# Unread matrix products issued on TensorE in the planned gaps of the first stage of a one-core layer kernel

## The chip, the core and the metric

The kernel runs on one core of one Trainium2 chip. The metric is the device time of one execution in microseconds (us), median of several runs. Every time below comes from the runs or from one profiled execution of the kernel before the change.

## What is computed

Sixteen sequences of 256 tokens with 128 features pass through four residual layers, each on a layer-normed input:

```
x = x + attn_a(layernorm(x))      # einsum('blmh,blhd->blhd'): the softmax row sums to 1, so it is
                                  # (x @ w_v.T + b_v) @ w_out.T + b_out
x = x + ffn(layernorm(x))         # 8 experts, top 2 of x @ gate_w, softmax over the two logits
x = x + ssm(layernorm(x))         # selective scan: 16 states, softplus delta, cumulative decays
x = x + ffn(layernorm(x))         # the same experts and gate again
```

The expert layer is, for each token, the sum over its two experts of the weight times `relu(x @ w1[e]) @ w2[e]`, with `w1[e]` 128x512 and `w2[e]` 512x128, all in float32.

## The kernel before

**Blocks and sets.** The 4096 tokens are 8 blocks of 512. `FIRST` groups them into sets for the first expert layer, ([0], [1], [2,3], [4,5], [6,7]), and `SECOND` into sets for the second. A set is routed as a whole: every token's row, scaled by its gate weight, is scattered by indirect DMA (`scatter`, POOL, line 807) to a slot of its expert in a DRAM buffer `slots`; the experts then read dense tiles from there, and `gather` (line 821) brings the results back by the same indices.

**What one block goes through before its first scan.** `attention`: TensorE (PE) transposes the loaded `xT` into token rows (`ps_b<-ident,xT`), ACT or DVE copies them to `x`, DVE takes the layer-norm statistics, POOL raises to the power -1/2 (`rstd`) and adds the bias (`x<-x,batt`), PE multiplies `xT` by the folded attention matrix (`ps_b<-wat,xT`), DVE adds the product to `x`. `gate`: statistics again, `xn`, PE transposes (`ps_b<-ident,xn`), copy to `xnT`, PE makes 8 gate logits per token (`ps_b<-gw_s,xnT`, 8 columns wide), copied to `lg`. `choose` and `route`: a row of small DVE operations finds the two experts (`oh`, `both`); PE counts the tokens ahead of each one (`ps_b<-both,before` and `ps_b<-both,onesb`, bf16); DVE makes the slot numbers (`rank`, `m`, `sf`, `to`), and POOL scatters. `experts`: a tile `xs` is fetched by SP, transposed on PE, copied to `xsT`; four up products `ps_b<-xsT,w_s` (192 columns in the first set) go through a ReLU on ACT or DVE to `h`; four down products accumulate in the one bank `ps_y<-h,w_s`; then copies, transposes and the write to `ys`. `mixer` holds the selective scan.

**Order.** No scheduler decides at run time. Every operation is recorded as a `Job` with a cost per engine; `Plan.forward` lists them on a model clock by ranks kept in `ORDER`, which gives each job an engine, a start and a buffer; `Plan.order` returns the jobs sorted by that start, and the loop at the end of `tile_layers` emits them. Each engine then works through its own list strictly in that order, waiting on semaphores where a value is not ready. In this plan's model a transposition takes PE 0.12 us and a float32 product of 128 columns 0.42 us.

**PSUM.** There are two banks of kind `b` of 512 columns, shared by nearly all short PE results, so a PE instruction often waits for the copy that empties its bank; one bank `y`, of which the experts use at most the first `NMAX` = 384 columns; and the banks `s`, `B`, `C` of the scan.

**Names the change touches.** `Plan.order` (the list it returns), the loop at line 1441 on, the bank `kinds["y"][0]`, and the constants `ones_d` (128x128, 1/128 everywhere) and `blank` (128x128, zero). Both constants are made by POOL at the start; no engine but PE gets another instruction or another order.

Of the kernel before, what the change touches and what calls it, by code (L numbers as in the profile page):

```python
# [21 lines left out]
TB = 512  # L22
# [12 lines left out]
JOIN = 2  # L35
ACC = 0
POOLED = (3,)
SUMS = 0
DENSE = ([], [])

# [144 lines left out]
class Plan:  # L185
# [160 lines left out]
    def order(self):  # L346

        self.prepare()
        d = zlib.decompress(base64.b85decode(ORDER))
        n = len(d) // 2  # L350
        assert n == len(self.jobs)
        at, rank = 0, []
        for lo, hi in zip(d[:n], d[n:]):
            at += int.from_bytes((lo, hi), "little", signed=True)
            rank.append(-at)
        end, start, way, buffer = self.made = self.forward(rank)
        for h, b in zip(self.homes, buffer):
            if b is not None:
                h.buffer = b
        order = sorted(range(n), key=lambda i: (start[i], i))  # L360
        return [(self.jobs[i], next(w for w in self.jobs[i].ways if w[0] == way[i])) for i in order]


@with_exitstack
# [229 lines left out]
def tile_layers(  # L594
# [33 lines left out]
    nc = tc.nc  # L628
    NTOK = xT.shape[1]
    NB = NTOK // TB  # L630
    NE, _, FF = w1.shape
    NFC = FF // P
# [15 lines left out]
    NMAX = max(c * n for _, c, n in every)  # L648
    MOST = -(-max(t * c * n for t, c, n in every) // P) * P

    plan = Plan()
# [6 lines left out]
    kinds = {}  # L658
# [78 lines left out]
    def either(*ways, extra=0.0, **order):  # L737

        made = []
        for e, name, a, k in ways:  # L740
            views = [x for x in (*a, *k.values()) if isinstance(x, View)]
            took = cost(e, name, views) + extra
            out = k["out"] if "out" in k else a[0]
            held = locking(e, name, out, [x for x in views if x is not out] + (
                [out] if sum(x is out for x in views) > 1 else []
            ))
            made.append((e, took, call(getattr(engines[e], name), a, k), held))
        _, _, a, k = ways[0]
        out = k["out"] if "out" in k else a[0]
        ins = [x for x in (*a, *k.values()) if isinstance(x, View) and x is not out]  # L750
        return plan.job(made, [out], ins, **order)
# [10 lines left out]
    def copy(out, in_, pool=False, **order):  # L762
        ways = [("ACT", "copy", (out, in_), {}), ("DVE", "tensor_copy", (out, in_), {})]
        if pool:
            ways.append(("POOL", "tensor_copy", (out, in_), {}))
        return either(*ways, **order)
# [61 lines left out]
    def filled(name, shape, value, dtype=F32):  # L828
        t = new(name, shape, dtype)
        G.memset(t, value)  # L830
        return t
# [18 lines left out]
    def load_experts():  # L850
# [21 lines left out]
        out=ident, in_=ident, pattern=[[-1, P]], compare_op=ALU.not_equal, fill=1.0, base=0,  # L872
        channel_multiplier=1,
    )
    ones_d = filled("ones_d", [P, P], 1.0 / P)
# [6 lines left out]
    blank = filled("blank", [P, P], 0.0)  # L882
# [5 lines left out]
    for q in range(3):  # L888
# [5 lines left out]
        out=before, in_=onesb, pattern=[[1, P]], compare_op=ALU.is_gt, fill=0.0, base=0,  # L894
# [5 lines left out]
        out=upto[:, P:L], in_=upto[:, P:L], pattern=[[-1, P]], compare_op=ALU.is_ge, fill=0.0, base=0,  # L900
# [388 lines left out]
    def mixer(b, r, m):  # L1289
# [31 lines left out]
        )  # L1321
        if SUMS:

# [24 lines left out]
        for n in range(0, NS, 2):  # L1348
# [29 lines left out]
            )  # L1378
            if n // 2 in POOLED:
                V.scalar_tensor_tensor(th, th, 1.0, pC, ALU.add, ALU.mult)  # L1380
# [61 lines left out]
    gap = sbuf.tile([1, 1], F32, tag="gap", name="gap")  # L1442
    last = None
    with tc.manual_schedule():
        for job, way in plan.order():
            if way[0] == "POOL":
                if job.key is not None and job.key == last:
                    nc.gpsimd.memset(gap, 0.0)
                last = job.key
            way[2]()  # L1450


    most = kept_s.tile([1, 1], F32, tag="most", name="most")
# [53 lines left out]
```

## Time and profile before

| | us |
|---|---|
| median of 3 runs | 724.63 (724.1 to 726.0) |
| the profiled execution's own time | 724.93 |
| its span, first to last instruction | 723.2 |
| first selective scan starts | 128.7 |
| first expert tile is transposed on PE | 54.64 |

Mean granted TensorE clock: 0.917 of full speed.

| stretch, us | PE busy | DVE busy | ACT busy | POOL busy | granted PE clock |
|---|---|---|---|---|---|
| 0 to 54.6 | 32.36 | 33.88 | 16.37 | 28.68 | 0.69 |
| 54 to 68.2 | 11.07 | 7.13 | 5.93 | 10.42 | 0.64 |
| 130 to 640 (510 us) | 462.36 | 462.57 | 395.51 | 305.04 | 0.94 |

How to read it: busy time is summed per engine; all kernel lines of the planned part show as line 710, the helper through which every recorded operation is called, so the groups are told apart by their tiles. A float32 product is recorded as two matmul records, a transposition as one. The granted clock is 1.00 or 0.50 at any moment; in between are means. From 0 to about 54 us the weights and the first tokens arrive, the first blocks are routed, and no expert runs yet; from 54 to 128 us the first experts run; from then on scans and experts overlap to the end.

### The profile page before, as it was taken

The numbers are of one execution on the slowest core, as the hardware profiler recorded it, in microseconds if no ns is written. First come the engines' busy times: TensorE is split into PE (matmuls) and PEld (weight loads), VectorE is DVE, ScalarE is ACT, GpSimd is POOL, SyncE is SP. The second block draws the span as 40 slices with busy tenths as digits, with TensorE's granted clock in tenths as the row PEclk, the third lists the DMA queues.
The fourth block names the chain that finished last, engine by engine and source line by source line (L and its number), as shares of the span: only waits on it lengthen the run. The fifth ranks groups of instructions, "written<-read, shape, count | busy, mean of one in ns | idle before, by whom it ended". The sixth has DMA issues, their size and how long they took to land. (4 is left out here: it accounts for less than half of the span.)

```text
span 723.2 us, 8786 instructions
## 1 busy us (share of the span) xinstructions
PE 624.5 (86%) x2598; PEld 390.6 (54%) x2598; DVE 554.6 (77%) x1038; ACT 487.7 (67%) x996; POOL 414.5 (57%) x490
## 2 busy tenths in 40 slices
PE   5477999799999769899888889887999999999970
PEld 4366877465645226555344554333555555578860
DVE  4765448999998798899999898998998998740120
ACT  2243538988867797679989668689867775355440
POOL 5367771397075458677953852864037787314743
PEclk9557999999999878799999999889999999999995
DMA  7931331221330001321122101110112512213342
GB/s 228 334 116 52 94 100 42 67 59 47 88 85 20 1 28 48 112 67 33 35 68 79 56 26 30 58 58 23 51 31 80 156 56 70 83 46 103 100 136 76
DMA packets 76373, 55.05 MB, mean 76 GB/s; under 512 B 8064, under 2 KB 69152, under 8 KB 76320
## 3 DMA queue, kind: packets, MB, share of 16 engines
q1 hardware_dynamic: 66464, 37.35, 17.8%
q0 software_dynamic: 8192, 16.79, 7.8%
q8 instruction: 22, 0.36, 0.2%
q10 hardware_dynamic: 1664, 0.29, 0.2%
q14 instruction: 31, 0.25, 0.1%
HBM read 27.09 MB, written 27.32 MB: 75 GB/s over the span
## 5 line engine op out<-in xcount | busy, mean ns | idle before, releaser
L710 PE MATMUL ps_b<-xsT,w_s 128*128 128x330 f32 (+3 forms) x640 | 211.0, 438 | 15.2 <-ACT h L710 6.8
L710 PE MATMUL ps_y<-h,w_s 128*128 128x330 f32 (+3 forms) x640 | 214.1, 425 | 3.4 <-ACT yT L710 2.2
L821 POOL DMA_INDIRECT yy<-ys,of x128 | 124.6, 973 | 100.7 <-DMA ys<-yr 38.5
L807 POOL DMA_INDIRECT slots<-row,to x128 | 126.7, 990 | 79.4 <-issue 22.1
L710 ACT ACTIVATE h<-ps_b 128x384 f32<-128x384 f32 (+2 forms) x234 | 110.2, 475 | 88.7 <-PE ps_b L710 85.4
L710 PEld LDWEIGHTS ps_b<-xsT,w_s 128*128 128x128 f32 x640 | 115.3, 197 | 74.1 <-ACT h L710 24.6
L710 DVE TENSOR_TENSOR_SCAN w<-decay,ps_B 128x1024 f32<-128x1024 f32 x64 | 145.8, 2279 | 0.2
L710 PEld LDWEIGHTS ps_y<-h,w_s 128*128 128x128 f32 x640 | 109.9, 195 | 44.8 <-issue 11.8
L710 ACT ACTIVATE th<-later,lneps,ha_s 128x512 f32<-128x512 f32 x128 | 100.1, 809 | 5.1 <-DVE th L710 2.9
L710 ACT ACTIVATE decay<-delta,nea 128x510 f32<-128x510 f32 x128 | 86.7, 714 | 4.7 <-DVE w L710 3.5
L710 DVE TENSOR_TENSOR ps_B<-du,ps_B 128x1024 f32<-128x1024 f32 x64 | 78.2, 1222 | 13.4 <-PE ps_B L710 13.2
L710 DVE SCALAR_TENSOR_TENSOR ps_C<-th,ps_C 128x1024 f32<-128x1024 f32 x56 | 68.2, 1219 | 6.9 <-PE ps_C L710 6.8
L710 PE MATMUL ps_s<-th,wsh_s 128*128 128x512 f32 x128 | 69.6, 636 | 3.8 <-POOL th L710 3.8
L710 DVE TENSOR_TENSOR th<-ps_C,w 128x1024 f32<-128x1024 f32 x56 | 67.9, 1213 | 0.2
L710 POOL TENSOR_TENSOR th<-th,th 128x1024 f32<-128x1024 f32 x20 | 47.2, 2360 | 29.5 <-DVE th L710 27.2
L710 POOL TENSOR_TENSOR rstd<-var,root 128x8 f32<-128x8 f32 (+1 forms) x20 | 28.2, 1412 | 52.1 <-DVE var L710 49.5
L710 PEld LDWEIGHTS <-sel 96*128 96x128 bf16 x256 | 25.9, 103 | 58.9 <-issue 48.3
L710 PE MATMUL ps_B<-pieces,sel 96*128 96x512 bf16 x128 | 42.0, 401 | 10.4 <-DVE w L710 10.3
L710 PE MATMUL ps_b<-ident,yT 128*110 128x128 f32 (+3 forms) x208 | 43.6, 279 | 2.8 <-ACT h L710 0.8
L710 PE MATMUL ps_b<-ident,xs 110*128 110x110 f32 (+3 forms) x208 | 38.9, 278 | 7.1 <-ACT h L710 3.2
L710 PE MATMUL ps_C<-pieces,sel 96*128 96x512 bf16 x128 | 41.7, 405 | 3.2 <-DVE th L710 3.0
L710 PEld LDWEIGHTS ps_b<-ident,xs 110*128 110x128 f32 (+3 forms) x208 | 26.6, 148 | 25.9 <-ACT h L710 8.5
(161 smaller groups left out, 810.6 us busy)
## 6 DMA issues: line engine op xcount, KB each, us to landing
slots<-blank SPq DMA_DIRECT2D x3, 1536.0 KB
xs<-slots SPq DMA_DIRECT2D x24, 192.0 KB
ys<-yr SPq DMA_DIRECT2D x24, 192.0 KB
w_s<-in_w SPq DMA_DIRECT2D x16, 256.0 KB
xs<-slots SPq DMA_DIRECT2D x24, 165.0 KB
ys<-yr SPq DMA_DIRECT2D x24, 165.0 KB
xT<-in_xT SPq DMA_DIRECT2D x8, 256.0 KB
slots<-row,to POOLq DMA_INDIRECT x128, 2.3
```

Of the source, the lines that this page charges most:

```text
L710: return lambda: f(*[real(x) for x in a], **{n: real(x) for n, x in k.items()})
L807: inst = nc.gpsimd.indirect_dma_start(out=real(out), out_offset=bass.IndirectOffsetOnAxis(ap=real(rows), axis=0), in_=real(in_), in_offset ...
L821: nc.gpsimd.indirect_dma_start(out=real(out), out_offset=None, in_=real(in_), in_offset=bass.IndirectOffsetOnAxis(ap=real(rows), axis=0), ...
```

## The change

`Plan.order` now returns, with each job, the time that PE stands idle just ahead of it on the model clock, for jobs that start before 110 us there. The loop emits, ahead of such a job, one 128x128x128 float32 product for each 0.24 us of that idle time: `ones_d` times `blank`, into the 128 columns of the bank `y` that no expert uses. Nobody reads it. While an expert's sum is open in the bank `y` (`summing`), none is emitted. Everything else keeps its order.

```diff
+WARM = 110.0
@@ Plan.order
         order = sorted(range(n), key=lambda i: (start[i], i))
-        return [(self.jobs[i], next(w for w in self.jobs[i].ways if w[0] == way[i])) for i in order]
+
+        idle, free = {}, 0.0
+        for i in order:
+            if way[i] == "PE":
+                idle[i] = start[i] - free if start[i] < WARM else 0.0
+                free = start[i] + self.jobs[i].took["PE"]
+        return [
+            (self.jobs[i], next(w for w in self.jobs[i].ways if w[0] == way[i]), idle.get(i, 0.0))
+            for i in order
+        ]
@@ tile_layers
     with tc.manual_schedule():
-        for job, way in plan.order():
+        spare, summing = kinds["y"][0][:, NMAX:TB], 0
+        for job, way, idle in plan.order():
+
+            for _ in range(0 if summing else int(idle / 0.24)):
+                nc.tensor.matmul(
+                    out=spare, lhsT=ones_d.real(), rhs=blank.real()[:, 0 : TB - NMAX],
+                    start=True, stop=True,
+                )
             if way[0] == "POOL":
                 if job.key is not None and job.key == last:
                     nc.gpsimd.memset(gap, 0.0)
                 last = job.key
             way[2]()
+            if way[0] == "PE" and any(h.kind == "y" for h in job.homes):
+                summing = (summing + 1) % NFC
```

In the built program this puts 132 products into PE's list, in 26 runs:

| ahead of | products |
|---|---|
| first transposition of the first block | 15 |
| the next transpositions and weight products | 3, 2, 1, 2 |
| `wat` products of the third and the fourth block | 6 and 22 |
| transposition of the first `xn` | 13 |
| its logits, and two weight products | 3, 1, 1 |
| counting products of the first set's route | 22 |
| transposition of the second `xn` | 15 |
| the next `xn` | 3, 1 |
| transposition of the fifth block's `xT` | 7 |
| the rest up to the first expert tile | 1, 3, 1, 1, 3 |
| first up products, first down product | 2, 2 |
| two later places, among the first set's experts | 1, 1 |

The first of them waits for POOL (the two constants). One of the later two carries the wait for ACT that the up product behind it had. DVE, ACT, POOL and SP have the same instructions in the same order as before.

## The prediction

> **What bounds the kernel now.** I read the page's slices first, then the stretches cut at the moments where the granted clock flips, then the order of time of PE alone, then of all engines. From 130 to 640 us DVE and PE are each busy 462 of 510 us and the change puts nothing there, so what counts is how much earlier or later the first expert stage hands over. The slices show where the clock is low:
>
> ```profile
> PE   5477999799999769899888889887999999999970
> PEclk9557999999999878799999999889999999999995
> ```
>
> A slice is 18 us. The third and fourth digits of PEclk cover 36 to 72 us, with PE busy in seven to nine tenths: there the clock may set the pace. Cut at the flips (duration, PE busy with records, then PEld, DVE, ACT, POOL, clock, DMA):
>
> ```profile
> 12.04:15.46 3.42, 2.94 (x13) 2.68 (x13) 2.10 (x10) 1.09 (x4) 3.00 (x4) 1.00 0.97 253
> 15.46:18.87 3.41, 1.41 (x13) 1.22 (x11) 3.33 (x9) 0.00 (x0) 2.44 (x2) 1.00 1.03 317
> ...
> 42.76:46.17 3.41, 3.41 (x18) 3.41 (x17) 1.40 (x11) 0.77 (x2) 2.81 (x5) 0.50 0.18 58
> 46.17:49.59 3.42, 2.70 (x17) 2.09 (x16) 2.46 (x19) 0.98 (x3) 1.29 (x3) 0.50 0.12 38
> 49.59:53.00 3.41, 3.39 (x23) 2.96 (x21) 2.78 (x16) 2.23 (x6) 1.93 (x2) 0.50 0.40 118
> 53.00:56.41 3.41, 1.91 (x10) 1.25 (x10) 3.37 (x15) 1.86 (x5) 1.88 (x3) 1.00 0.01 3
> ...
> 63.24:66.65 3.41, 3.41 (x12) 3.41 (x11) 1.64 (x11) 0.76 (x2) 2.07 (x4) 0.50 0.18 58
> ```
>
> The clock moves in steps of 3.41 us and each step follows the one before. Half turns to full after nearly full PE stretches (49.59, 63.24), full is lost after 1.41 and 1.91 us busy; later 2.04 us (from 128.09) holds it and 1.82 (from 131.51) loses it. The stretch from 42.76 is full of gate products 8 columns wide and does not raise it: narrow products hardly count. Up to 15.46 the view says 1.00, but single transpositions last as long there as at 0.50 later (four in 1.08 us at 4.31, four in 1.09 at 27.60); I take that part as half clock too.
>
> ```profile
> 19.26 2.07 PE L710 MATMUL ps_b<-wat,xT 128*128 128x128 f32 x8 [2.39 <-DVE x L710]
> 24.44 2.08 PE L710 MATMUL ps_b<-wat,xT 128*128 128x128 f32 x8 [3.11 <-DVE x L710]
> 27.60 1.09 PE L710 MATMUL ps_b<-ident,xn 128*128 128x128 f32 x4 [1.08 <-DVE x L710]
> ...
> 34.72 0.19 PE L710 MATMUL ps_b<-both,before 128*128 128x40 bf16 x1 [1.64 <-DVE p L710]
> ...
> 37.91 1.12 PE L710 MATMUL ps_b<-ident,xn 128*128 128x128 f32 x4 [2.92 <-ACT xn L710]
> ...
> 43.41 3.42 PE L710 MATMUL ps_b<-gw_s,xnT 128*128 128x8 f32 x16
> 46.68 1.09 PE L710 MATMUL ps_b<-ident,xT 128*128 128x128 f32 x4
> ...
> 54.64 0.39 PE L710 MATMUL ps_b<-ident,xs 96*128 96x96 f32 x2 [0.68 <-ACT x L710]
> ```
>
> In brackets stands PE's idle time ahead: these are the gaps the new products go into, and they are not the plan's gaps.
>
> **Price of one product.** It is two records. At half clock 16 records take 3.42 us: 0.213 each, 0.43 a product. At full clock the 192-column records of 72 to 78 us come in pairs 0.325 apart, 0.163 each; by columns 128/192 of that is 0.108, and four transpositions of 128 columns in 0.60 us (104.89), the last one 0.27 long, give 0.11. The bounds are 0.11 and 0.163 a record; I take 0.11, the same width: 0.22 a product, 29 us for 132.
>
> **Walk through the front, clock held at full.**
> - 15 ahead of the first block: they start when `blank` is written (2.28 + 0.20) and, at half clock until one 3.41 us step is full, end between 7.2 and 8.9 instead of the 4.31 at which the first block landed. What hides it is ACT, which makes its first copy of a block only at 9.94, behind its table load, and 3.46 us of idle DVE ahead of 10.55: 0 to +0.5. Without that cover it would be +3 to +4.6.
> - 3, 2, 1, 2 and 6: 1.3 us or less each, in gaps of 0.3 to 2.4: nothing.
> - 22 ahead of the fourth block's `wat`: the third block's eight records take 0.9 from 19.26; 20.2 + 4.9 = 25.1 against 24.44, but at full clock these eight end at 26.1 against 26.5. Nothing.
> - 13 ahead of the first `xn`: 26.1 + 2.9 = 29.0 against 27.60. Transpositions 0.6 against 1.09, eight gate records 1.05 against 1.87: logits at 31.2 as before. Even.
> - 22 ahead of the route: from 32.5 to 37.4 in a gap of 1.64, so the count starts 2.7 late. Behind it on DVE stand `rank`, the slot numbers and the next block's `xn`; 0.73 us of DVE idle ahead of `rt` absorbs some, so scatters start 2.0 late (39.6) and, at 1.27 each, end at 49.7 instead of 47.7. SP's fetch, queued behind them, goes from 48.96 to 51. PE asked for that tile at 54.64, so this is hidden; about 2 us of slack are left.
> - 15 and 3 ahead of the next `xn`: 40.9 against 37.91, 3.0 late. From there PE is the pace: 36 records up to 46.83, all at half clock before. At full the 16 gate records take 1.8 instead of 3.42; the last logits come at 46.5 + 0.2 against 46.86. Regained.
> - 7 ahead of the fifth block's `xT` (46.68, no gap before): 1.6 us. The copy that empties its bank, and with it the last product of the second route, comes 0.55 later (DVE `rank` 49.95 against 49.42). Behind that on DVE are statistics, for which POOL waits at 51.07; its three additions stretch DVE, and the first up product (55.54) moves as much. The 3, 1, 1, 3, 2 and 2 after it lie in gaps of 0.3 to 0.7: nothing.
>
> Sum: +0.55, up to +1.0 with the first item.
>
> **What the clock gives in the first experts.** Rows of PE from 57 to 68:
>
> ```profile
> 57.04 1.01 PE L710 MATMUL ps_y<-h,w_s 128*128 128x192 f32 x2 [0.58 <-ACT h L710]
> 60.46 1.65 PE L710 MATMUL ps_b<-xsT,w_s 128*128 128x192 f32 x4 [0.41 <-ACT xsT L710]
> 62.69 1.01 PE L710 MATMUL ps_y<-h,w_s 128*128 128x192 f32 x2 [0.58 <-ACT h L710]
> 64.77 3.57 PE L710 MATMUL ps_b<-xsT,w_s 128*128 128x192 f32 x14
> ```
>
> Between 57.04 and 62.69 the chain is four down records, two transposed tiles, four up records, with an ACT copy after each group; at 0.163 instead of 0.32 a record it is 3.8 instead of 5.65 long. From 62.69 to 68.17 twenty wide records run, bound by PE; at full 3.3 to 3.6 (the ReLUs of 0.49 now pace them) instead of 5.5. Together 3.8. PE is then the pace until 91 and POOL's scatters, closed up from 79.6 to 97, have 4.6 us of waits before 79.6 to give back, so it carries to the first scan. Net with the clock held: 0.55 - 3.8 = -3.2.
>
> **Where the clock is lost again.** A long dip of wide products costs one step at half rate.
> - Dip A: the 6 products end near 16.8 and PE waits until 19.26, 2.4 us. A step that holds most of it has 1.0 to 1.4 us of work, like the one that lost the clock at 18.87. About half of all positions of the step do. Then 3.4 us of the 22 products run at half: +1.7.
> - Dip B: from 42.0 to 46.5 there are some 1.1 us of wide records; the rest are gate products. Steps starting from 41.7 to 44.0 lose it: two in three. Then the 7 products cost up to 3.0 instead of 1.6, transpositions and gate records double: the second route comes 1.6 to 3.3 late instead of 0.55, and the experts may start at half clock, which takes up to a third off the 3.8.
>
> Held -3.2; A alone -1.5; B alone +2.2 - 3.8 x 0.85 = -1.0; both about +0.7, with the late end of B +2.5.
>
> The Trainium skill, page "TensorE: Matmul & The Clock Gate", section "Why this matters for your kernels", asks for no PE gaps over about 3 us to keep full clock. By it a gap of 2.4 us would be harmless, dip A would not exist, and B, which is busy, neither: 724.9 - 3.2 = 721.7 on the profiled execution. This trace differs: full clock was lost at 18.87 with no gap above 2.39 us, so I keep both dips.
>
> **Forecast.** The clock is raised early, lost once, mostly at B: -1.0. The profiled execution, 724.93 (723.2 span and 1.7 around it), becomes 723.9; it stood 0.3 above the median of 724.63, so the median becomes 723.6. Own range: 722.3 to 725.5. Chance 0.44.
>
> **Rivals.**
> - *Clock never lost* (-3.2, median 721.4). For it: 2.04 us of work held it at 128.09, and the runs of 15, 22 and 7 are dense. Against: the two dips. Chance 0.23.
> - *Slower: products that arrive at half rate in front of work that is ready.* Place: the 7 ahead of the fifth block's `xT`, where PE had no gap. If the clock falls at B's early end after A, gates, 7 products and transpositions all run at half, the second route leaves near 53 instead of 49.4, and the experts begin cold: +1.7 + 3.3 - 2.5 = +2.5, median 727.1. It decides once DVE's second `rank` comes more than 3.8 late. For it: the gate row; against: the 7 products themselves fill the next step. Chance 0.22.
> - *Gain swallowed behind*: POOL's scatters to 97 and the gathers after them keep their times, 724.6. Against: POOL's 2.97 us wait at 75.05, on DVE work paced by PE. Chance 0.08.
> - *Zeros do not raise the clock*: the change does not do what it says. No row shows a product of zeros. All runs at 0.43: the runs of 22, 13, 22, 15 and 7 would exceed their gaps by about 20 us, median 745. Chance 0.03; left outside the range.
>
> A measurement of this kernel tells about 0.3% (2.2 us) from no change. Faster: most of the first rival and a little of the forecast, 0.27. Slower: most of the second, the last, and the forecast's upper tail, 0.25. The same: 0.48. Range: the prices run from -3.2 (-3.6 with the first ReLU bound) to +2.5 (+3 with +0.5 from the first item): 721.0 to 727.5.
>
> **What would show it.** Clock at full from 5 to 9 us on and DVE's first copy at 8 to 9.5, with ACT's first copy still near 10; the first count near 37.4 and first scatter near 39.6; last logits near 46.7 (two or more later means a lost step); second `rank` at 50 to 52; first up product at 56 to 58; 9 us from there to where it took 12.6. The prediction is wrong if the clock stays low through the dense runs, if ACT's first copy moves, or if the first scan does not move with the experts.

## The result and the profile after

A correction first: the change section speaks of 26 runs of products; its table lists all there are, and they are 25.

| | us | executions |
|---|---|---|
| before, beside the change | 726.18 (722.27 to 729.79) | 19 |
| the change | 726.24 (718.98 to 734.03) | 19 |
| ratio | 0.9994, 95% interval 0.9972 to 1.0017 | |
| predicted | 723.6 (721.0 to 727.5), "same" at 0.48 | |

No difference that this measurement can tell. (Ratios, here and below, leave out disturbed executions, so they can differ a little from the quotient of two medians.) The execution of the change that was profiled took 721.01 us (span 719.3), one of its fastest; before's took 724.93. So the two traces differ by 3.9 us where the medians don't, and part of the reading below is where those 3.9 come from.

The slices of the change's page, busy tenths and granted clock (a slice is 18 us):

```profile
PE   8898999799999769899788899788999999999970
PEclk9999999999999979799999999899999999999995
```

The first four digits of the clock were 9 5 5 7: the zero products do raise the clock, and it stays up. PE is busier in the front (8 8 9 8 for 5 4 7 7), as it must be. Order of time of PE in the change (start, duration, operation, idle time ahead of it):

```profile
2.54 5.62 PE L1460 MATMUL ps_y<-blank,ones_d 128*128 128x128 f32 x30 [2.54 <-POOL blank L721]
8.00 0.60 PE L721 MATMUL ps_b<-ident,xT 128*128 128x128 f32 x4
...
15.89 1.50 PE L1460 MATMUL ps_y<-blank,ones_d 128*128 128x128 f32 x12
19.77 1.50 PE L721 MATMUL ps_b<-wat,xT 128*128 128x128 f32 x8 [2.38 <-DVE x L721]
21.07 6.40 PE L1460 MATMUL ps_y<-blank,ones_d 128*128 128x128 f32 x44
27.31 1.06 PE L721 MATMUL ps_b<-wat,xT 128*128 128x128 f32 x8
...
34.78 5.18 PE L1460 MATMUL ps_y<-blank,ones_d 128*128 128x128 f32 x44
39.79 0.18 PE L721 MATMUL ps_b<-both,before 128*128 128x40 bf16 x1
...
46.84 1.95 PE L721 MATMUL ps_b<-gw_s,xnT 128*128 128x8 f32 x16
48.65 1.81 PE L1460 MATMUL ps_y<-blank,ones_d 128*128 128x128 f32 x14
50.29 0.60 PE L721 MATMUL ps_b<-ident,xT 128*128 128x128 f32 x4
```

Four transpositions take 0.60 us from 8.00 on (1.08 before), sixteen gate products 1.95 instead of 3.42. But the operation behind a long run has no bracket: it waited for nothing but the run. The count stood at 34.72 before and stands at 39.79, directly behind 22 unread products.

Two steps of the clock in the same trace (duration, PE busy and records, then PEld, DVE, ACT, POOL, clock):

```profile
17.00:20.44 3.44, 1.06 (x10) 0.87 (x9) 3.36 (x14) 0.00 (x0) 1.22 (x1) 1.00 1.11 357
20.44:23.85 3.41, 3.41 (x19) 3.41 (x18) 1.26 (x12) 0.00 (x0) 2.66 (x2) 0.50 1.15 348
...
44.30:47.70 3.40, 3.40 (x29) 3.02 (x28) 3.04 (x16) 1.77 (x5) 2.75 (x7) 1.00 0.18 58
47.70:51.15 3.45, 3.45 (x32) 3.34 (x32) 2.41 (x19) 0.59 (x3) 2.79 (x7) 1.00 0.12 38
```

The step with 1.06 us of work is dip A of the prediction, and one step at half clock follows it. Dip B, the gate products around 45, kept full clock here.

How far the same operations lie from their time before, in us (minus is earlier; two executions of the change, two of the refit described below, one of the late version of experiment 9):

| operation | before at | change | change again | refit | refit again | late alone |
|---|---|---|---|---|---|---|
| ACT's first copy | 9.94 | +0.8 | +1.7 | 0.0 | -0.1 | 0.0 |
| first logits copied | 31.27 | +2.2 | +1.5 | -1.5 | -1.6 | 0.0 |
| first count, PE | 34.72 | +5.1 | +4.4 | -1.5 | -1.6 | 0.0 |
| last logits copied | 46.86 | +2.0 | +1.3 | -4.6 | -4.9 | 0.0 |
| second `rank`, DVE | 49.42 | +2.7 | +2.0 | -3.7 | -5.0 | 0.0 |
| first up product | 55.54 | +2.6 | +1.9 | -3.2 | -4.5 | +1.1 |
| fourth expert tile | 68.17 | -1.0 | -0.3 | -6.8 | -8.1 | -2.5 |
| first scan | 128.7 | -0.5 | +0.3 | -6.4 | -7.7 | -2.2 |
| DVE at 600 | 600 | -5.0 | -0.7 | -13.2 | -12.2 | -0.3 |
| end of the span | 723.2 | -3.9 | -0.5 | -12.8 | -11.5 | +0.4 |

The front ends 2 to 2.6 us late, the experts give 3.6 back where the clock holds through them (2.1 in the second execution, which lost a step at 63.3), and what reaches the first scan is -0.5 and +0.3. The other 4.5 us of the profiled execution arise behind the first scan, 2.7 of them between 243 and 256 us, where before stood at half clock and the change did not. That stretch before and in the change:

```profile
243.00:256.00 13.00, 11.42 (x30) 4.98 (x29) 9.65 (x17) 10.04 (x19) 3.80 (x3) 0.82 0.01 2
```

```profile
243.00:256.00 13.00, 10.09 (x28) 3.75 (x28) 12.33 (x20) 12.92 (x24) 3.15 (x4) 1.00 0.00 1
```

Before's execution stood at half clock for 58.0 us between 130 and 680, the change's for 41.0, its second one for 47.8. That differs between executions of one kernel, and the medians say that on the whole it gave this kernel nothing.

### The profile page after: what moved, and what is told of

The parts are those of the page before. It is cut to its first block, busy times and chain, and to the rows that moved or that the text cites. A ratio compares the mean times of both kernels' runs of the same rounds, so it can differ in the third digit from the quotient of the medians.

```text
span 719.3 us, 9311 instructions
## 1 busy us (share of the span) xinstructions
PE 635.6 (88%) x2862; PEld 406.8 (57%) x2862; DVE 556.3 (77%) x1038; ACT 487.5 (68%) x996; POOL 414.1 (58%) x490
## 5 line engine op out<-in xcount | busy, mean ns | idle before, releaser
L721 PE MATMUL ps_b<-xsT,w_s 128*128 128x330 f32 (+3 forms) x640 | 207.0, 430 | 14.3 <-ACT h L721 6.3
L721 PE MATMUL ps_y<-h,w_s 128*128 128x330 f32 (+3 forms) x640 | 211.4, 420 | 2.8 <-ACT yT L721 2.0
L721 PEld LDWEIGHTS ps_b<-xsT,w_s 128*128 128x128 f32 x640 | 112.3, 192 | 72.6 <-ACT h L721 23.4
L721 PEld LDWEIGHTS ps_y<-h,w_s 128*128 128x128 f32 x640 | 108.1, 192 | 43.5 <-issue 11.3
L721 PE MATMUL ps_s<-th,wsh_s 128*128 128x512 f32 x128 | 67.5, 618 | 4.0 <-POOL th L721 3.8
```

What stands on the lines that cost most here:

```text
L721: return lambda: f(*[real(x) for x in a], **{n: real(x) for n, x in k.items()})
```

## The experiments

All of them keep the kernel's own computation whole and alter only the unread products. A list of run lengths takes the place of the rule, in the order of the table in the change section:

```diff
+RUNS = (15, 3, 2, 1, 2, 6, 22, 13, 3, 1, 1, 22, 15, 3, 1, 7, 1, 3, 1, 1, 3, 2, 2, 1, 1)
-        spare, summing = kinds["y"][0][:, NMAX:TB], 0
+        spare, summing, runs = kinds["y"][0][:, NMAX:TB], 0, iter(RUNS)
-            for _ in range(0 if summing else int(idle / 0.24)):
+            for _ in range(0 if summing or idle < 0.24 else next(runs)):
```

With this list the program is the change's; each experiment names the numbers it alters. Experiments 1 to 4, 7 and 8 are one execution each.

**1. No products ahead of the count.** The 22 in the twelfth place become 0.

> The 22 unread products ahead of the first set's route are left out, the other 110 stay. In the changed kernel's profile the count started at 39.79 instead of 34.72, and the second rank on DVE at 52.1 instead of 49.4. Theory of the prediction (this run's delay is hidden or regained): second rank, first up product (58.1) and fourth-tile transposition (67.15) stay within 0.5. Rival (an overrun is passed on to everything behind it): count near 36.5 to 37.5, second rank 2 to 3 us earlier, near 49.5, first up near 55.5, fourth tile near 64.5. In both the clock may be lost for a step in the gap that opens.

724.78 us, beside 726.14 for before. The count came at 37.33 instead of 39.79, the first scatter 1.7 us earlier. The second `rank` came at 51.28 instead of 52.12, the first up product at 57.28 instead of 58.13, the fourth tile at 66.30 instead of 67.15: 0.85 us earlier all the way, although this execution lost a further step of clock, at 38.4, in the gap that was left open. That is between the two expectations, and by itself no more than executions differ: in the change's second one the second `rank` stood at 51.40. The same execution's own first logits are the better base. From there to the last logits the two profiles of the change and that of experiment 2, which have this run, gain 0.24, 0.24 and 0.23 us on before, this one 1.48: the run costs some 1.2 us. So it is not wholly hidden behind SP's fetch: it also holds up PE's own next work, the transpositions and gates of the second set.

**2. No products ahead of the fifth block's `xT`.** The 7 in the sixteenth place become 0.

> The 7 unread products ahead of the fifth block's transposition are left out. Theory of the prediction: they stand in front of ready work, so that transposition comes 1.6 earlier after the last gate products than in the changed kernel (1.8 from the start of its gate row to it instead of 3.45), and second rank and first up 0.5 to 1.6 earlier. Rival (the route waits for DVE anyway): second rank and first up move less than 0.3. If the clock is lost for a step behind the gate products, this shows in the rows and the first up product comes 1 to 2 later.

719.94 us. The transposition started 1.81 us behind the start of its gate row, as the theory had it. Second `rank` 50.53 (1.6 us earlier than in the change), first up product 56.95 (1.2), fourth tile 65.96, first scan 127.0 (1.2), with one step lost at 49.4. Not all of it is the seven's: this execution kept full clock over dip A, and its last logits, ahead of the seven, were 0.9 earlier already. From there to the second `rank` the change loses 0.7 (+2.0 to +2.7 against before, and as much in its second profile and in experiment 1), this kernel nothing (+1.1 and +1.1). So they did stand in front of ready work, at 0.7.

**3. The refit.** Every long run cut to what the idle stretch held in the profile of before, the short one of dip A lengthened:

```diff
-RUNS = (15, 3, 2, 1, 2, 6, 22, 13, 3, 1, 1, 22, 15, 3, 1, 7, 1, 3, 1, 1, 3, 2, 2, 1, 1)
+RUNS = (10, 3, 2, 1, 2, 10, 19, 8, 3, 1, 1, 9, 12, 3, 1, 2, 1, 3, 1, 1, 3, 2, 2, 1, 1)
```

> The same places, with 102 products: run lengths set by the gaps measured at full clock (10 instead of 15 at the start, 10 instead of 6 and 19 instead of 22 around the third block's weight products, 8 instead of 13, 9 instead of 22, 12 instead of 15, 2 instead of 7). Theory (gain 3.8 from the clock in the first experts, loss from overruns in front): clock held at full from about 10 us on, second rank at 48 to 50, first up product at 54 to 56, fourth-tile transposition at 63 to 65.5, first scan 2.5 to 4 earlier than the 128.7 before the change. Rival (the front is set by DVE and POOL, not by what PE does): second rank and first scan as in the changed kernel within 0.5 (52.1 and 128.2).

725.89 us, beside 726.14 for before. The front gained more than either expectation had: second `rank` at 44.58, fourth tile at 60.25, 7.9 us earlier than before, first scan at 123.1, 5.6 earlier. The distance stayed at 5.5 up to 578 us and was gone by 600. There the order of time of DVE shows two small operations drawn out:

```profile
576.86 1.72 DVE L722 SCALAR_TENSOR_TENSOR rt<-rt,var 128x4 f32<-128x4 f32 x1
...
586.40 3.15 DVE L722 TENSOR_SCALAR xn<-x,rstd,mean 128x128 f32<-128x128 f32 x2
```

The first takes 0.16 us in before and 0.15 in the refit's profile of experiment 10, the pair 0.60 in both. Each ended with or just behind a POOL operation beside it (`x<-x,yy` from 577.29 to 578.56, `th<-th,th` from 586.84 to 589.19); and the clock was at half from 590.1 for 6.8 us. Experiments 10 and 12 show that this belongs to one execution and not to the refit.

**4. Late alone.** Only the 14 products of the last eight places (3, 1, 1, 3 up to the first expert tile, 2, 2, 1, 1 among the first experts); all others 0.

> Only the last 8 runs (14 products), from the transpositions just ahead of the first expert tile on; nothing before 50 us. Theory: the front is as before the change (second rank 49.4, first up 55.5); whether the 14 products hold the clock depends on a nearly full step at half clock just before: if they do, the fourth-tile transposition comes at 64.5 to 66 (68.17 before) and the first scan 2 to 3.5 earlier; if not, both as before within 0.7. Rival (the early products are needed to have any full clock there): clock half from 50 to 64 and no gain.

719.92 us. The front is before's, clock included (half from 20.6 to 54.7), then full through the experts: fourth tile at 66.12, first scan at 126.9, 1.8 us earlier than before and more than the change's 132 products reach. At the fourth tile it is the 3.6 us of the first experts less 1.6 by which the first up product, behind most of the 14, comes later.

**5 and 6. Refit and late, timed.** The kernels of 3 and 4.

> The refitted run lengths again, timed. Theory (the gain at the first scan, 5.6 in the first look, travels to the end unless a chance event in the later part takes some of it): first scan at 122.5 to 125, median 2 to 6 us below the kernel before, ratio 0.992 to 0.997. Rival (something behind the first scan sets the end whatever the front does, as in the first look, where 723.1 to 724.2 came out): median within 1.5 us of the kernel before.

> Only the last 14 products again, timed. Theory: the front as before the change up to 53, first scan about 1.8 earlier than 128.7, median 1 to 3 us below the kernel before, between that one and the refitted one. Rival (the early products decide, and the first look had a lucky later part): first scan as before within 0.7 and median within 1 us of the kernel before.

When these were timed, together with experiments 7 and 8, every kernel was slower by a tenth, before too: 796.22 us (23 executions). Refit 794.92, ratio 1.0002 (0.9969 to 1.0036); late 799.55, ratio 0.9959 (0.9911 to 1.0008). Both intervals hold 1, and late's median lies above before's while its ratio lies below 1: no difference is shown, and neither expectation is decided. What POOL's gathers waited for, in the late kernel's profile of experiment 4 and in this one (us in total, times, longest):

```profile
POOL yy L833 <- DMA ys<-yr: 38.0, 4, 16.8
```

```profile
POOL yy L833 <- DMA ys<-yr: 70.4, 6, 22.8
```

The gathers waited longer for the experts' results in DRAM, and the first scan lay at 146.0 (refit) and 146.1 (late): there the front's pace no longer decides. A later measurement, with before at 726.53, ran on the same chip, so it was no lasting property of the chip. What it was stays open.

**7. Narrow.** The same 132 products, 8 columns wide instead of 128.

```diff
-        spare, summing, runs = kinds["y"][0][:, NMAX:TB], 0, iter(RUNS)
+        spare, summing, runs = kinds["y"][0][:, NMAX : NMAX + 8], 0, iter(RUNS)
-                    out=spare, lhsT=ones_d.real(), rhs=blank.real()[:, 0 : TB - NMAX],
+                    out=spare, lhsT=ones_d.real(), rhs=blank.real()[:, 0:8],
```

> The 132 products of the change with 8 columns instead of 128: the same number of weight loads and records, hardly any columns. Theory (the clock counts streamed columns, not busy time): the records take the time of the gate records (0.21 at half), the clock stays at half through the runs of 22 and 15, the route's count comes at 42 to 50, and the fourth-tile transposition later than 68.2, first scan 4 to 14 later than before. Rival (any busy PE raises the clock): full clock from 6 to 9 us on, count near 40 and fourth tile near 67 as in the changed kernel.

820.44 us beside the 796. The order of time of PE:

```profile
2.54 6.57 PE L1461 MATMUL ps_y<-blank,ones_d 128*128 128x8 f32 x30 [2.54 <-POOL blank L722]
8.96 1.09 PE L722 MATMUL ps_b<-ident,xT 128*128 128x128 f32 x4
```

and by stretches (columns as above):

```profile
20.00:40.00 20.00, 20.00 (x97) 20.00 (x95) 10.29 (x53) 1.26 (x3) 4.80 (x4) 1.00 1.03 325
40.00:60.00 20.00, 19.88 (x98) 19.56 (x99) 5.71 (x43) 3.81 (x12) 3.38 (x3) 1.00 0.00 1
```

PE is busy nearly all the time, its weight loads (PEld) too, and the clock is not raised: four transpositions still take 1.09, and the first change of the clock comes at 83.9 us (the 1.00 before a trace's first change means nothing). A record of 8 columns takes 0.21 us there (30 in 6.57), as much as one of 128. So busy time alone does not raise the clock; the same 132 products with 128 columns do, as the gate products at 43.4 of before had suggested. The count came at 57.14, later than either expectation, the first up product at 86.62 and the first scan at 171.4, 25 us behind the 146 of the refit and late, which is about what the whole lost.

**8. Whole.** The rule of the change over the whole plan, 419 products instead of 132.

```diff
-WARM = 110.0
+WARM = 1000.0
```

> The rule of the change for the whole plan instead of the first 110 us: 419 products in 96 runs, 287 of them behind the first scan. Theory (the plan's gaps are not the chip's): fewer half-clock steps between 130 and 640 than the 42 to 55 us of the kernels seen, but products in front of ready work; front as in the changed kernel (first scan 126.5 to 128.5), end within 6 us of it on either side. Rival (the later half-clock steps are what separates 719 from 727 us): almost no half clock between 130 and 640 and the end below 717.

816.01 us, 20 above before's median in that measurement and above the highest of its 23 executions (806.28); both expectations failed. The mean clock was 0.943 (late in the same measurement 0.895), and the first scan lay at 146.3 as in refit and late. The loss comes behind it: from 146 to 345 us PE is busy for 178.5 us instead of late's 167.4, DVE for 165.9 instead of 167.9. More clock, more busy PE, less done. Which runs of products stood in front of ready work was not followed.

**9, 10 and 11. Late, refit and the change side by side**, before at 726.35 us (722.34 to 732.95, 23 executions).

> The 14 unread products in front of the shared expert and the experts alone, on the chip that this call gets, with the change itself and the refit beside it. Theory (these products hold the clock through the first experts for 3.8 us of plain time, and cost nothing that the first scan sees): ratio to the kernel before 0.996 to 0.998 where the kernel before takes about 726 us, and not above the change itself. Rival (the later half-clock steps, which fall differently from execution to execution, swallow 2 us): 0.999 to 1.001, interval across 1.

> The runs of the change cut to what the idle stretches of the plan held in the profile before (10, 10, 19, 8, 9, 12, 2 in place of 15, 6, 22, 13, 22, 15, 7). Theory (the first scan starts 5 us earlier and the distance lasts): ratio 0.992 to 0.996. Rival (what the single look showed: the distance is given back behind the second scans, at a half-clock step and at small DVE operations beside POOL): 0.998 to 1.001.

> The change as it is, beside the other two. Theory: ratio 0.998 to 1.001, as in the first comparison. Rival (the later half-clock steps decide): outside 0.996 to 1.004.

| | us | executions | ratio to before |
|---|---|---|---|
| late | 722.43 (718.29 to 727.52) | 12 | 0.9942 (0.9905 to 0.9979) |
| refit | 715.21 (711.45 to 720.32) | 6 | 0.9845 (0.9791 to 0.9899) |
| the change | 726.37 (717.51 to 737.8) | 12 | 0.9969 (0.9928 to 1.0010) |

The change is again level: its ratio lies just below the expected 0.998, its interval holds that and 1. Late is ahead of before by 0.2 to 1.0%, a little more than expected. The refit is faster by more than its theory asked. PE in the refit's profile:

```profile
2.53 4.63 PE L1461 MATMUL ps_y<-blank,ones_d 128*128 128x128 f32 x20 [2.53 <-POOL blank L722]
6.96 0.90 PE L722 MATMUL ps_b<-ident,xT 128*128 128x128 f32 x4
...
15.15 2.40 PE L1461 MATMUL ps_y<-blank,ones_d 128*128 128x128 f32 x20
19.02 1.16 PE L722 MATMUL ps_b<-wat,xT 128*128 128x128 f32 x8 [1.48 <-DVE x L722]
20.02 4.41 PE L1461 MATMUL ps_y<-blank,ones_d 128*128 128x128 f32 x38
24.26 1.09 PE L722 MATMUL ps_b<-wat,xT 128*128 128x128 f32 x8
...
31.05 2.27 PE L1461 MATMUL ps_y<-blank,ones_d 128*128 128x128 f32 x18
33.20 0.18 PE L722 MATMUL ps_b<-both,before 128*128 128x40 bf16 x1
...
42.13 1.20 PE L1461 MATMUL ps_y<-blank,ones_d 128*128 128x128 f32 x4
43.12 1.06 PE L722 MATMUL ps_b<-ident,xT 128*128 128x128 f32 x4
```

Ten products raise the clock too (full from 7.6), ten carry it over dip A, and the count stands at 33.20, 1.5 us before its old place. At 43.12 four transpositions take 1.06: this execution lost the clock at dip B, at 41.7.

**12. The refit a third time.**

> The refitted runs (10, 3, 2, 1, 2, 10, 19, 8, ...) once more, by themselves. They were 11 us ahead of the kernel before in one comparison (715.2 against 726.4), level with it in a single look (725.9 against 726.1) and level on the chip where every kernel takes about 796 us. Theory (the front is 5 to 7 us earlier in every one of these and the rest falls with the half-clock steps): ratio 0.985 to 0.995 where the kernel before takes about 726 us, the first scan 5 to 7 us earlier in the profile. Rival (the 715 us belonged to that one chip): ratio 0.997 to 1.002, with the first scan still 5 to 7 us earlier.

716.97 us (710.24 to 724.38, 9 executions), before 726.53 (14): 0.9861 (0.9817 to 0.9905). The first scan lay at 121.0, 7.7 us earlier than before's. The refit beats before and the change.

## Why the prediction came out as it did

The forecast "same" came true, and the mechanism was right in outline: products of zeros raise the clock within the first run, it is lost in dips, the experts speed up, the products' overruns eat it. The forecast stood at -1.0 us against its own base; the ratio of 0.9994 is -0.4 us of 726, its interval -2.0 to +1.2, so neither the size nor the sign of the forecast is refuted or shown by the times alone. Of the 2.6 us between 723.6 and 726.24, 1.6 is the base: three executions gave before a median of 724.63, nineteen 726.18.

That it came so near is in part luck. The overruns were to move the first up product by +0.55. In the change's second profile, which had lost no step by then, they moved it by +1.9, and a step lost inside the experts, which the forecast did not have, took another 1.5; in the first profile the step was lost at dip A and not at B.

By its own steps:

- **Price of a product: right.** At full clock 44 records take 5.18 us and 12 take 1.50 in the rows above: 32 more in 3.68, 0.115 each, where 0.11 was taken. At half clock six records took 1.49 us (in the refit, at 45.98), 0.83 at full.
- **The 15 ahead of the first block: the step that failed.** It was given 0 to +0.5: "What hides it is ACT, which makes its first copy of a block only at 9.94, behind its table load". That took the table load for a cover that stands still. It is not one: with the 15 products it starts behind DVE's first copy, which waits for the transposition that the products delay. Before:

```profile
8.64 1.28 ACT L710 ACT_TABLE_LOAD   x1 [8.64 <-DMA wso_s<-in_w_so]
```

  The change's second profile:

```profile
9.56 0.69 DVE L721 COPY x<-ps_b 128x512 f32<-128x512 f32 x1 [4.97 <-PE ps_b L721]
...
10.31 0.66 PE L721 MATMUL ps_b<-ident,xT 128*128 128x128 f32 x4
```

```profile
10.34 1.28 ACT L721 ACT_TABLE_LOAD   x1 [10.34 <-DMA bso_s<-in_b_so]
11.63 1.07 ACT L721 COPY x<-ps_b 128x512 f32<-128x512 f32 x2
```

  The narrow version, which tells DVE's copy from PE's next transposition:

```profile
10.09 0.69 DVE L722 COPY x<-ps_b 128x512 f32<-128x512 f32 x1 [5.50 <-PE ps_b L722]
...
10.86 1.28 ACT L722 ACT_TABLE_LOAD   x1 [10.86 <-DVE x L722]
...
11.20 1.09 PE L722 MATMUL ps_b<-ident,xT 128*128 128x128 f32 x4
```

  In all eight profiles in which DVE's first copy ends later than 8.5 us, the load starts 0.08 us behind that end (10.25 and 10.34, 10.78 and 10.86 above). In the other six, before among them, it starts 0.1 us behind ACT's last DMA issue, which ends at 8.5 to 8.6. In five executions with the run of 15 ACT's first copy moved by +0.8 to +1.7, and DVE's work from there on by 0.5 to 1.4. With ten products it moved by -0.1 to +0.2. "The prediction is wrong if ACT's first copy moves", its last paragraph said, and here it was.
- **22 and 13 ahead of `wat` and `xn`, "nothing" and "even": right as a walk, wrong as a price.** In the change's second profile, which kept the clock over dip A, the first logits lie at +1.5, where the run of 15 had put them. But with 19 and 8 in their place the refit's first logits lie at -1.5: of the 3.0 between the two, the shorter first run explains 1.7 (DVE's +1.4 and -0.2 at 24 us), and the other 1.3 is put down to these two runs, which are what the two lists differ in from there to the logits. The walk compared each place with its old time; the place it should have been compared with is where the same work could stand at full clock.
- **22 ahead of the count: sized right (2.7 late; 2.9 measured, 2.2 to 5.1 and 1.5 to 4.4), cover half right.** Scatters and the fetch had room (fetch 53.88, first tile at 56.85). What was missing is PE's own next work: some 1.2 us by experiment 1.
- **15 and 3, "regained": right against before, and here most was given away.** From the last transposition of `xn` to the last logits the change falls back from +3.9 to +2.0 (first profile) and from +3.1 to +1.3 (second). The refit has them at -4.6 and -4.9: the front at full clock is worth nearly 5 us up to there, which the prediction put at none, since it let the products take it.
- **7 ahead of the fifth `xT`: right.** Forecast 0.55 at `rank`; between last logits and second `rank` 0.7 was lost in both profiles, and nothing without the seven.
- **First experts, 3.8: right.** First up product to fourth tile 12.63 before, 9.02 in the change's first profile, the refit and the late version: 3.6.
- **Dips: one of the two, the other one.** "About half of all positions" for dip A: of five executions with a run of 6 there, three lost it, two did not. B was lost in the one without the seven and in all four profiles of the refit; in the change's two profiles it held. So the likeliest case, "mostly at B", was the wrong dip. A cost the 1.7 that was forecast (from +0.5 to +2.2 at the logits, and from +0.9 to +2.6 in experiment 1).
- **The gain carries to the first scan: right**, within 0.6 us, so the rival *gain swallowed behind* fell too. What the prediction left out lies behind it: from execution to execution the half-clock steps between 130 and 680 us move the end by more than the whole change was to bring.

Of the rivals, *clock never lost* would have given -3.2; the change's second profile comes nearest, with a single step lost up to 130 us (at 63.3), and has -0.3 at the fourth tile. Of the 2.9 that are missing there 1.5 is that step (10.50 us through the first experts instead of 9.02) and 1.4 is overruns. That the overruns weigh more than this comparison shows, the refit tells: it lost a step too, and with shorter runs its fourth tile lies 5.8 us or more ahead of the change's. The slower rival (727.1) was to decide with a second `rank` over 3.8 us late; it came 2.7 and 2.0 late. *Zeros do not raise the clock* fell with the first profile.

The Trainium skill (page "TensorE: Matmul & The Clock Gate", section "Why this matters for your kernels") asks for no PE gaps over about 3 us. Keeping to that was not enough here, a second time: the change lost the clock at 20.44 after a step whose longest gap was 2.38 us.

That the refit gains 10 to 11 us at the median and only 6.4 to 7.7 at its first scan is not wholly explained. In both profiles the rest comes at 240 to 300 us, in the first near 490 too, where half-clock steps of before's execution are missing (34.1 and 41.0 us at half between 130 and 680 against 58.0). The mean clock and the span of every execution, from which its time at half clock follows, say the same of more than the profiles. It was 117 us in before (23 executions of experiments 9 to 11), 76 in the change (12) and 67 and 70 in the refit (6 and 9). The profiles put 44, 3 and 3 to 7 of that ahead of 130 us. So behind the front the change has as much half clock as before, some 72 us, and the refit 60 to 67. Executions of one kernel, change or refit, took 0.4 to 0.5 us longer for each us more at half clock; by that the refit's 5 to 12 us would be worth 2 to 6, an estimate that covers the rest. Why an earlier front should lose fewer steps was not tried.

## What to carry to other kernels

Filling idle time of PE to hold its clock paid here where the filler is shorter than the idle time that the chip shows, at full clock; a plan's model of the gaps is not that, and each product too many stands in front of ready work. Size each run from the profile, keep it dense and wide in the long dips, and ask of every engine named as a cover what releases it: one that is released by work behind the products, directly or through another engine, covers nothing. Where a few half-clock steps decide, time a dozen executions of each version: single profiles of one program lay 3.4 us apart here, and of the refit 14.

## What was not expected of the hardware

- A float32 record of 8 columns takes PE 0.21 us at half clock, as long as one of 128, and counts next to nothing towards the clock: in the narrow version PE was busy for 20.00 of the 20 us from 20 to 40, and the clock was not raised up to 83.9 us.
- The grid of 3.41 us stands differently in each execution: full clock came at 6.8 and 8.7 us in two executions of the same program, and DVE's work at 12 us lay 0.9 us apart.
- A DVE operation on 128x4 took 1.72 us instead of 0.16 beside a POOL operation, and a pair on 128x128 3.15 instead of 0.60, in one execution of the refit and not in the next. Before has such a place as well: the same operation took 1.21 us at 15.48, beside POOL's `x<-x,batt`.
- Every kernel took a tenth longer in one measurement than in the others, with longer waits for DMA, on a chip that ran at the usual time afterwards.
- ACT's table load of 1.28 us did not run in the idle time ahead of its first copy: with the 15 products it started only 0.08 us behind DVE's first copy.
